# Two graph layers on one core: the adjacency transposed by DMA, an earlier load, and a new timetable

## The chip, the core and the metric

The kernel runs on one NeuronCore of a Trainium2 chip. Five engines with a queue each take part: TensorE (PE in the profile, its weight loads PEld) for matmuls and transposes, VectorE (DVE), ScalarE (ACT), GpSimd (POOL), and SyncE (SP), which here only issues DMAs. Each engine runs its own queue in order; an instruction that waits holds up everything behind it on that engine. The metric is the device time of one execution in microseconds, as a median of several runs. The profile is one execution of its own.

## What is computed

64 independent graphs, each with 256 nodes of 256 features and an integer adjacency matrix, go through two layers. The first is attention with relations: the softmax of q k is masked by each of four values of the adjacency, and each mask has its own values v. The second is a graph attention network with two attention steps that share the mask adjacency > 0. Both layers end in a feed-forward block. Cut to what matters here:

```python
# layer 0
scores = q @ k.T / sqrt(dh)                       # 8 heads of 32
attn = softmax(scores, axis=-1)
for r in range(4):
    out += (attn * (adj == r)) @ (src @ Wv[r])
x = ln(src + out @ Wo)
x = ln(x + gelu(x @ W1) @ W2)
# layer 1, the attention step twice
e = leaky_relu(Wh1 + Wh2.T)
h = softmax(where(adj > 0, e, -9e15), axis=1) @ Wh
x = ln(x + h);  x = ln(x + relu(x @ w_ff1) @ w_ff2)
```

## The kernel before

One graph is the unit of work: its 256 rows are two blocks of 128 partitions, and all its steps are methods of the class Graph, gathered by name in `operations`. All weights stay in SBUF. The matmuls are float32; the attention weights are used with the key nodes on the partitions, so the adjacency is needed transposed, too.

What sets the order is a timetable written out by hand. The dictionary PLACES gives each step a place; graph g has its steps at `g * PERIOD + place`, and the last lines of the kernel sort the steps of all 64 graphs by place and run them in that order, which is then each engine's queue order. A place is no time: it only ranks steps. With a period of 60 and places from about -14 to 270, steps of five graphs stand between each other. What is called place 33.7 below is a place taken modulo the period. A tile framework adds the semaphore waits and hands out the buffers: two of each front tile (`fp`), three PSUM tiles of the tag "mm", one PSUM bank for each of four heads' scores (`ps_s`).

The steps that the change and the prediction speak of:

- `load` (L134 to L139): the DMAs of x (xin) and of the adjacency (adi) of a graph, on SP. Graph 0's are issued first of all (L141), then come 34 DMAs of weights and vectors on the same queue (L142 to L177); all other loads come from the timetable. `y` (L433 to L435) loads x again for the residual, `store` (L524) writes the result; both are on SP as well.
- `cast` (L304, POOL) turns the integer adjacency into bfloat16 (adb). `jT` (L306 to L311) transposes it with four 128x128 transposes on TensorE into a PSUM tile, and `jTc` (L315, ACT) copies that to adT in SBUF. `mask0` to `mask4` (L326 to L331, POOL) compare adT with the relations; mask4 is the mask of the second layer.
- `xT` and `xTc` (L217, L221) transpose x; `qk0`, `qk1` (L337), `v00` to `v11` (L353) are the projections, in two halves m of four heads each.
- `s0`, `s1` (L370): scores of four heads as matmuls of 32 rows each[...]. Then for each head `max` (L375, DVE), `exp` (L383, ACT), `rec` (L388, DVE), `nrm` (L393, POOL), `eT` (L399, TensorE, back into the scores' PSUM bank), `es` (L404, ACT), `pm` (L408, DVE, the product with three masks), `pl` (L413, POOL, that with the last mask). `po0`, `po1` (L424) are the products with v, in matmuls of 32 columns.
- `wo` (L444), `ya`, then a layer norm of `st1` (DVE), `rt1` (L242, POOL) and `ln1` (L247, L251, DVE). The feed-forward block of the first layer: `aT`, `au0` to `au3` (L270), `ax0` to `ax3` (L277, ACT), `ad0` to `ad7` (L284), `ae` (L288, DVE), and its norm `st2`, `rt2`, `ln2`.
- `hT` (L217) transposes the result of ln2 for the second layer: `ga0`, `ga1` (L454), two attention steps (names in h and z), and a second feed-forward block with names in b, ended by `ln4` and `store`.

[...]

Of the kernel before, what the change touches and what calls it, by code (L numbers as in the profile page):

```python
# [12 lines left out]
BF16 = mybir.dt.bfloat16  # L13
# [4 lines left out]
P = 128  # L18
# [4 lines left out]

PERIOD = 60.0
PLACES = {
    "load": -13.81, "cast": -13.72, "xT": -4.66, "xTc": -4.31, "jT": -2.14, "jTc": 3.89, "qk0": 10.32,
    "qkc0": 15.38, "mask3": 18.4, "qk1": 19.52, "qkc1": 33.51, "mask0": 40.4, "v00": 41.99, "s0": 44.39,
    "max01": 45.28, "exp01": 46.53, "max00": 48.41, "exp00": 48.86, "vc00": 49.3, "max02": 50.12,
    "y": 51.75, "v10": 52.12, "max03": 52.91, "vc10": 53.45, "exp03": 53.62, "exp02": 54.7, "rec00": 55.23,
    "rec02": 56.39, "v11": 56.45, "rec03": 56.54, "mask1": 56.72, "mask2": 56.92, "nrm00": 57.02,  # L30
    "eT00": 57.47, "nrm03": 58.18, "vc11": 58.18, "es00": 58.93, "rec01": 61.34, "v01": 61.37,
    "nrm02": 62.41, "eT03": 62.5, "nrm01": 62.52, "pl00": 62.83, "eT02": 63.75, "pm00": 63.87, "eT01": 65,
    "es03": 65.49, "pl03": 66.47, "es02": 67.28, "vc01": 68.87, "es01": 69.64, "pl02": 70.44, "pm03": 70.48,
    "pm02": 71.62, "pm01": 72.69, "s1": 73.61, "pl01": 74.01, "max11": 74.9, "exp11": 76.55, "max10": 77.17,
    "exp10": 78.46, "max12": 78.53, "max13": 79.42, "rec11": 80.21, "po0": 80.41, "exp12": 82.35,
    "exp13": 82.95, "mask4": 83.04, "rec10": 83.25, "nrm10": 83.92, "rec12": 84.3, "rec13": 84.35,
    "nrm11": 86.8, "nrm13": 87.83, "nrm12": 88.42, "eT13": 89.04, "es13": 90.24, "eT11": 91.08,
    "eT10": 92.68, "oT0": 93.27, "es10": 95.39, "pm13": 95.55, "yb": 97.25, "eT12": 98.12, "pl13": 98.77,
    "es11": 99.15, "pl11": 99.64, "pm10": 101.39, "es12": 101.49, "pm11": 102.06, "pm12": 102.56,
    "pl10": 103.39, "pl12": 105.68, "po1": 105.84, "oT1": 109.02, "wo": 112.3, "ya": 114.97, "st1": 116.77,  # L40
    "rt1": 117.4, "ln1": 121.15, "aT": 123.26, "aTc": 126.48, "au0": 127.81, "au1": 127.98, "ax0": 130.26,
    "ax1": 130.8, "ad0": 134.18, "au2": 137.15, "ax2": 138.43, "au3": 139.03, "ax3": 139.66, "ad1": 140.92,
    "ad2": 141.77, "ad3": 145.91, "ad4": 145.97, "ar": 146.32, "ad5": 146.89, "ad6": 148.4, "ad7": 148.7,
    "ae": 150.15, "st2": 150.31, "rt2": 153.25, "ln2": 156.6, "hT": 159.27, "hTc": 159.41, "ga0": 159.97,
    "gac0": 160.28, "ga1": 161.37, "gac1": 161.98, "ipA": 162.06, "zA": 162.47, "zlA": 163.61,
    "zmA": 164.43, "zxA": 165.33, "zeA": 171.75, "zdA": 173.45, "h10": 176.82, "h1c0": 177.52,
    "h11": 177.66, "h1c1": 181.08, "ipB": 181.31, "zB": 181.33, "zlB": 185.72, "zmB": 187.61, "zxB": 187.79,
    "zeB": 189.32, "zdB": 191.16, "h2": 192.43, "h2a": 194.37, "st3": 195.73, "rt3": 199.46, "ln3": 203.48,
    "bT": 207.02, "bTc": 208.89, "bu0": 213.43, "bx0": 215.34, "bu1": 217.76, "bd0": 217.96, "bx1": 218.81,
    "bu2": 219.87, "bd1": 220, "bx2": 222.24, "br": 222.74, "bu3": 222.91, "bd2": 223.5, "bx3": 227.29,  # L50
    "bd3": 231.33, "bd4": 236.75, "bd5": 238.2, "bd6": 243.84, "bd7": 244.4, "be": 252.56, "st4": 253.99,
    "rt4": 257.67, "ln4": 265.08, "store": 269.91,
}


def _row(ap, n):

    return bass.AP(tensor=ap.tensor, offset=ap.offset, ap=[[0, P], [1, n]])
# [8 lines left out]
def kernel(  # L67
# [12 lines left out]
    nc = tc.nc  # L80
    B, N, D = x.shape
# [6 lines left out]
    C = N // P  # L88
# [4 lines left out]
    const = ctx.enter_context(tc.tile_pool(name="const", bufs=1))  # L93
# [8 lines left out]
    def mm_tile(shape, name, dt=F32):  # L102
        return ps_mm.tile(shape, dt, tag="mm", name=name)
# [4 lines left out]

    ident = const.tile([P, P], F32, name="ident")
    make_identity(nc, ident)  # L110
    ident_h = const.tile([P, P], BF16, name="ident_h")
    nc.vector.tensor_copy(ident_h, ident)
    nhalf = const.tile([P, 2], F32, name="nhalf")
    nc.vector.memset(nhalf, -0.5)
    negc = const.tile([P, 1], F32, name="negc")
# [2 lines left out]
    def weight(w, name):  # L118
        k, n = w.shape[0] // P, w.shape[1]
        t = const.tile([P, k, n], F32, name=name)  # L120
        nc.sync.dma_start(t, w.rearrange("(k p) n -> p k n", p=P))
        return t

    def rowvec(v, n, name):
        t = const.tile([P, n], F32, name=name)
        nc.sync.dma_start(t, _row(v, n))
        return t
# [6 lines left out]
    def load_front(g):  # L134
        xin = fp.tile([P, C, D], F32, tag="xin", name=f"xin{g}")
        nc.sync.dma_start(xin, x[g].rearrange("(c p) d -> p c d", p=P))
        adi = fp.tile([P, C, N], I32, tag="adi", name=f"adi{g}")
        nc.sync.dma_start(adi, adj[g].rearrange("(c p) d -> p c d", p=P))
        return xin, adi  # L139

    loaded = {0: load_front(0)}  # L141
# [8 lines left out]
    for m in range(KD):  # L150
        for k in range(KD):
            nc.sync.dma_start(
                wv[:, k, m], Wv[:, k * P:(k + 1) * P, m * P:(m + 1) * P].rearrange("r p n -> p r n"))
        nc.sync.dma_start(
            bv_r[:, m], bass.AP(tensor=bv.tensor, offset=bv.offset + m * P, ap=[[0, P], [D, R], [1, P]]))
    wo, bo_r = weight(Wo, "wo"), rowvec(bo, D, "bo_r")
    g1_r, be1_r = rowvec(g1, D, "g1_r"), rowvec(beta1, D, "be1_r")
    w1, b1_c = weight(W1, "w1"), colvec(b1, FF, "b1_c")
# [131 lines left out]
    class Graph:  # L290
# [12 lines left out]
            self.adb = fp.tile([P, C, N], BF16, tag="adb", name=f"adb{self.g}")  # L303
            nc.gpsimd.tensor_copy(self.adb, self.adi)  # L304

        def adj_product(self):  # L306
            self.ap = mm_tile([P, C, N], f"aT_ps{self.g}", BF16)
            for jc in range(C):
                for ic in range(C):
                    nc.tensor.transpose(self.ap[:, jc, ic * P:(ic + 1) * P],  # L310
                                        self.adb[:, ic, jc * P:(jc + 1) * P], ident_h)  # L311

        def adj_copy(self):
            self.adT = fp.tile([P, C, N], BF16, tag="adT", name=f"adT{self.g}")
            nc.scalar.copy(self.adT, self.ap)  # L315

        def mask(self, r):

# [207 lines left out]
        def operations(self):  # L526

            g, ops = self.g, {}
# [5 lines left out]
            ops["cast"] = self.cast  # L534
            ops["xT"] = lambda: self.xt.product(self.xin)
            ops["xTc"] = self.xt.copy
            ops["jT"] = self.adj_product
            ops["jTc"] = self.adj_copy
            for r in range(R + 1):
                ops[f"mask{r}"] = lambda r=r: self.mask(r)  # L540
            for m in range(KD):
# [56 lines left out]
    for g in range(B):  # L598
        ops = Graph(g).operations()
# [34 lines left out]
```

## Time and profile before

| | |
|---|---|
| timed runs, us | 4013.57, 4013.96, 4015.55; median 4013.96 |
| profiled execution: span, us | 4008.9 |
| granted TensorE clock | 0.994 of full speed |
| distance between the jT steps of two graphs in the middle, us | 61.31 |
| DMA | 80.00 MB, 20 GB/s over the span |
| load of xin or adi, median us to landing | 2.9 and 3.2 |
| four bfloat16 transposes of L310, per record | 219 ns, 256 records |
| copy of L315 on ACT | 586 ns, 64 of them |
| loads of a function table on ACT | 381, 1283 ns each |

A line of the profile names the engine, the source line, the operation, what it writes and reads, the shape, and how many there are, then the busy time and the mean of one; behind the bar stands the idle time of the engine just before, and what ended it. In a timeline, the first column is the start and the second the duration in microseconds, and equal instructions that follow each other are merged into one line with their number; a bracket gives the idle time before it and its cause. A float32 matmul appears as two MATMUL records, a transpose as one. Matmuls are pipelined, so the duration of one record (some 380 ns for 256 columns) is longer than the distance to the next (216 ns); the distance between starts is what counts. The busy slices cut the span into 40 equal parts of about 100 us, each with a digit in tenths.

### The profile page before, as it was taken

To read this page: it belongs to the slowest core of one execution; us is meant where nothing else is said; L and a number is where in the kernel's file an instruction comes from. 1 tells how busy PE (TensorE), PEld (TensorE's weight loads), DVE (VectorE), ACT (ScalarE), POOL (GpSimd) and SP (SyncE) were. 2 spreads that over 40 slices of the span, in tenths; PEclk is the share of its full clock that TensorE was granted. 3 is DMA by queue.
4 is the path that set the end of the run, shared out by engine and by line. 5 is a ranking of instruction groups with operands and counts; after the bars stand their busy time and mean duration, and the time that the engine had idled before them with its cause. 6 is when DMAs were issued, how large, how long until landed. Compare 5 with 4: busy or idle time off the path is not lost.

```text
span 4008.9 us, 67819 instructions
## 1 busy us (share of the span) xinstructions
PE 3945.9 (98%) x26136; PEld 3026.2 (75%) x26136; DVE 2788.9 (70%) x5129; ACT 2321.4 (58%) x5693; POOL 2154.9 (54%) x2374
## 2 busy tenths in 40 slices
PE   6999999999999999999999999999999999999998
PEld 4677777777777777777777777777777777777776
DVE  4677667676776776777767767767777677677675
ACT  3565565565655655656656556556566565565563
POOL 4555555555555555555555555555555555555551
PEclk8999999999999999999999999999999999999999
DMA  4000000000000000000000000000000000000000
GB/s 112 11 22 12 22 16 18 22 12 22 22 12 22 22 12 22 13 21 22 12 22 22 11 22 22 12 22 12 22 22 12 22 22 12 22 22 12 22 6 11
DMA packets 82404, 80.00 MB, mean 20 GB/s; under 512 B 8224, under 2 KB 81568, under 8 KB 82080
## 3 DMA queue, kind: packets, MB, share of 16 engines
q1 hardware_dynamic: 82080, 75.66, 6.2%
q8 instruction: 206, 3.38, 0.4%
q14 instruction: 118, 0.97, 0.1%
HBM read 58.87 MB, written 16.78 MB: 19 GB/s over the span
## 4 chain that ended last, share of the span: by engine, by line
PE 60%; ACT 16%; DVE 10%; issue 6%; POOL 4%; POOLq 0%; DVEq 0%; ACTq 0%
PE v_ps L353 11%; PE ffb_po L284 10%; ACT e L383 6%; PE po L424 6%; PE ffa_ps L270 6%; PE ffb_ps L270 5%; ACT L383 4%; ACT L277 4%; POOL e L393 4%; PE s L370 3%; PE ga_wps L454 3%; DVE pm L408 3%; PE wo_ps L444 3%; PE h_ps L503 3%; PE qk_ps L337 3%
## 5 line engine op out<-in xcount | busy, mean ns | idle before, releaser
L393 POOL TENSOR_SCALAR e<-e,rden 128x256 f32<-128x256 f32 x1024 | 588.4, 589 | 896.6 <-ACT xT L221 597.9
L408 DVE TENSOR_TENSOR pm<-rel,s 128x1536 f32<-128x1536 uint8 x512 | 887.0, 1743 | 55.9 <-ACT es L404 55.8
L413 POOL TENSOR_TENSOR pm<-rell,es 128x512 f32<-128x512 bf16 x512 | 609.4, 1201 | 225.2 <-ACT es L404 225.2
L383 ACT ACTIVATE e<-s,nmax 128x256 f32<-128x256 f32 x1024 | 474.0, 473 | 318.2 <-DVE nmax L375 316.7
L242 POOL TENSOR_TENSOR rs_x<-ve_x,nhalf 128x2 f32<-128x2 f32 x256 | 183.7, 718 | 691.4 <-DVE ve_x L238 673.7
L284 PE MATMUL ffb_po<-f,ffb_h 128*128 128x256 f32 x2048 | 524.1, 384 | 0.0
L284 PE MATMUL ffa_po<-w,ffa_h 128*128 128x256 f32 x2048 | 486.5, 385 | 0.0
L353 PE MATMUL v_ps<-wv,xT 128*128 128x512 f32 x1024 | 484.6, 596 | 0.0
L270 PE MATMUL ffb_ps<-ffb_T,f 128*128 128x256 f32 x2048 | 475.4, 380 | 0.7 <-ACT ffb_T L221 0.7
L424 PE MATMUL po<-pm,v 128*32 128x256 f32 x8192 | 469.8, 381 | 0.0
L270 PE MATMUL ffa_ps<-ffa_T,w 128*128 128x256 f32 x2048 | 463.2, 379 | 0.0
L284 PEld LDWEIGHTS ffb_po<-f,ffb_h 128*128 128x128 f32 x2048 | 374.3, 190 | 95.4 <-issue 29.6
L284 PEld LDWEIGHTS ffa_po<-w,ffa_h 128*128 128x128 f32 x2048 | 373.8, 190 | 90.0 <-issue 46.8
L404 ACT COPY es<-s 128x512 f32<-128x512 f32 x512 | 301.8, 590 | 222.5 <-PE s L399 181.4
L270 PEld LDWEIGHTS ffa_ps<-ffa_T,w 128*128 128x128 f32 x2048 | 384.2, 190 | 49.8
L375 DVE TENSOR_REDUCE nmax<-s 128x2 f32<-128x512 f32 x512 | 333.5, 683 | 111.5 <-PE s L370 111.5
L270 PEld LDWEIGHTS ffb_ps<-ffb_T,f 128*128 128x128 f32 x2048 | 375.5, 191 | 44.6 <-ACT ffb_T L221 1.1
L424 PEld LDWEIGHTS po<-pm,v 128*32 128x32 f32 x8192 | 253.4, 110 | 197.6 <-issue 44.1
L388 DVE RECIPROCAL rden<-den 128x2 f32<-128x2 f32 x512 | 69.3, 156 | 353.4 <-ACT e L383 353.3
L360 DVE TENSOR_TENSOR v<-v_ps,bv_r 128x512 f32<-128x512 f32 x256 | 175.6, 686 | 199.4 <-PE v_ps L353 191.2
L331 POOL TENSOR_SCALAR rel<-adT 128x512 uint8<-128x512 bf16 x192 | 310.1, 1625 | 0.0
L399 PEld LDWEIGHTS s<-ident,e 128*128 128x128 f32 x2048 | 245.4, 141 | 62.3 <-issue 18.7
(108 smaller groups left out, 6362.9 us busy)
## 6 DMA issues: line engine op xcount, KB each, us to landing
xin<-in_x_dram SPq DMA_DIRECT2D x64, 256.0 KB, 2.9
adi<-in_adj_dram SPq DMA_DIRECT2D x64, 256.0 KB, 3.2
y<-in_x_dram SPq DMA_DIRECT2D x64, 256.0 KB, 3.7
out_dram<-ffb_res SPq DMA_DIRECT2D x64, 256.0 KB, 2.2
w<-in_L_gnn_W_dram SPq DMA_DIRECT2D x2, 1024.0 KB, 8.6
f<-in_L_gnn_w_ff_dram SPq DMA_DIRECT2D x2, 1024.0 KB, 9.3
wv<-in_L_gnn_Wv_dram SPq DMA_DIRECT2D x4, 256.0 KB, 5.1
bv_r<-in_L_gnn_bv_dram SPq DMA_DIRECT2D x2, 256.0 KB, 5.5
```

Source lines behind the costliest of these rows:

```text
L270: nc.tensor.matmul(p[:, f - f0, :], self.wa[:, k, f * P:(f + 1) * P], self.x.t[:, k, :], start=(k == 0), stop=(k == KD - 1))
L284: nc.tensor.matmul(self.p[:, c, :], self.h[:, f, c * P:(c + 1) * P], self.wb[:, f, :], start=(f == 0), stop=(f == KF - 1))
L331: nc.gpsimd.tensor_scalar(self.rel[:, r], self.adT, float(r), None, op0=ALU.is_equal)
L353: nc.tensor.matmul(p, self.xt.t[:, k, jc * P:(jc + 1) * P], wv[:, k, m].rearrange("p r n -> p (r n)"), start=(k == 0), stop=(k == KD - 1))
L375: nc.vector.tensor_reduce(self.nmax[m, h], self.s4[m][h].rearrange("p (c n) -> p c n", c=C), AX.X, ALU.max, negate=True)
L383: nc.scalar.activation(e[:, ic, :], self.s4[m][h][:, ic * N:(ic + 1) * N], AF.Exp, bias=self.nmax[m, h][:, ic:ic + 1], accum_out=self.den[ ...
L393: nc.gpsimd.tensor_scalar(e[:, ic, :], e[:, ic, :], self.rden[m, h][:, ic:ic + 1], 1.0, op0=ALU.mult, op1=ALU.mult)
L399: nc.tensor.transpose(self.s4[m][h][:, jc * N + ic * P:jc * N + (ic + 1) * P], self.e[m, h][:, ic, jc * P:(jc + 1) * P], ident)
L404: nc.scalar.copy(self.es[m, h], self.s4[m][h])
L408: nc.vector.tensor_tensor(self.pm[m, h], self.rel.rearrange("p r c n -> p r (c n)"), bc(self.s4[m][h], [P, R - 1, C * N]), ALU.mult)
L413: nc.gpsimd.tensor_tensor(self.pm_l[m, h], self.rel_l.rearrange("p c n -> p (c n)"), self.es[m, h], ALU.mult)
L424: nc.tensor.matmul(po[hp, :], self.v[m][:, jc, r, hp], w, start=(r == 0 and jc == 0), stop=(r == R - 1 and jc == C - 1))
```

## The change

Three things change at once.

1. The four transposes on TensorE and the copy on ACT become two DMA transposes on SP, each from one block of 128 rows of adb straight to its columns of adT. The step jTc no longer exists, nor does the bfloat16 identity matrix.
2. x and the adjacency of graph 1 are loaded ahead of wo, that is, after the weights of the projections and before all later ones.
3. All 175 places of the timetable are new. No step but jT and jTc changes what it does.

```diff
-    ident_h = const.tile([P, P], BF16, name="ident_h")
-    nc.vector.tensor_copy(ident_h, ident)
...
+    loaded[1] = load_front(1)
     wo, bo_r = weight(Wo, "wo"), rowvec(bo, D, "bo_r")
...
-        def adj_product(self):
-            self.ap = mm_tile([P, C, N], f"aT_ps{self.g}", BF16)
-            for jc in range(C):
-                for ic in range(C):
-                    nc.tensor.transpose(self.ap[:, jc, ic * P:(ic + 1) * P],
-                                        self.adb[:, ic, jc * P:(jc + 1) * P], ident_h)
-
-        def adj_copy(self):
+        def adj_transposed(self):
             self.adT = fp.tile([P, C, N], BF16, tag="adT", name=f"adT{self.g}")
-            nc.scalar.copy(self.adT, self.ap)
+            for ic in range(C):
+                nc.sync.dma_start_transpose(out=self.adT[:, :, ic * P:(ic + 1) * P], in_=self.adb[:, ic, :])
...
-            ops["jT"] = self.adj_product
-            ops["jTc"] = self.adj_copy
+            ops["jT"] = self.adj_transposed
```

Of the timetable, the places that the prediction speaks of, before and after, modulo the period of 60 where they stand in it:

| step | before | after | | step | before | after |
|---|---|---|---|---|---|---|
| load | 46.2 | 40.9 | | s1 | 13.6 | 13.6 |
| store | 29.9 | 52.9 | | po0 | 20.4 | 14.9 |
| cast | 46.3 | 49.3 | | ad7 | 28.7 | 29.9 |
| jT | 57.9 | 55.3 | | ae | 30.2 | 31.2 |
| y | 51.8 | 58.2 | | pm13 | 35.5 | 36.5 |
| mask3 | 18.4 | 10.6 | | ln2 | 36.6 | 33.7 |
| s0 | 44.4 | 46.8 | | hT | 39.3 | 35.5 |
| po1 | 45.8 | 48.3 | | ln4 | 25.1 | 29.4 |

Between s1 and po0 stood ad0, au2, au3 and qk1 before; now nothing does. In the order before, pm13 stood on DVE between st2 and ln2; now ln2 follows st2 directly.

## The prediction

> **What bounds the kernel now.** I read the busy table first, then the busy slices, then TensorE's timeline of one graph in the middle, then the start, then the Vector engine (DVE) beside a place where TensorE waits.
>
> ```profile
> PE 3945.9 (98%) x26136; PEld 3026.2 (75%) x26136; DVE 2788.9 (70%) x5129; ACT 2321.4 (58%) x5693; POOL 2154.9 (54%) x2374
> ...
> PE   6999999999999999999999999999999999999998
> ```
>
> TensorE is busy in every slice but the first and the last; no other engine is over 70%. A busy TensorE need not be at its peak, so the next view is the timeline of TensorE around one graph, with start, duration, and how many records were merged:
>
> ```profile
> 2009.27 0.60 PE L217 MATMUL ffb_T_ps<-ident,ffa_res 128*128 128x128 f32 x4
> 2009.70 1.89 PE L284 MATMUL ffa_po<-w,ffa_h 128*128 128x256 f32 x8
> 2011.43 1.47 PE L399 MATMUL s<-ident,e 128*128 128x128 f32 x12
> ...
> 2017.06 0.60 PE L399 MATMUL s<-ident,e 128*128 128x128 f32 x4
> 2017.67 0.94 PE L217 MATMUL hT_ps<-ident,ffa_res 128*128 128x128 f32 x4
> 2018.45 1.89 PE L270 MATMUL ffb_ps<-ffb_T,f 128*128 128x256 f32 x8
> ...
> 2041.69 0.39 PE L310 MATMUL aT_ps<-ident_h,adb 128*128 128x128 bf16 x4
> 2041.92 1.08 PE L284 MATMUL ffb_po<-f,ffb_h 128*128 128x256 f32 x4
> 2042.84 0.38 PE L466 MATMUL gb_ips<-ident,gb_wh 128*128 128x128 f32 x2
> ...
> 2055.25 1.15 PE L370 MATMUL s<-kT,qT 32*128 32x256 f32 x16
> 2056.33 1.13 PE L284 MATMUL ffa_po<-w,ffa_h 128*128 128x256 f32 x4
> 2057.30 3.62 PE L270 MATMUL ffa_ps<-ffa_T,w 128*128 128x256 f32 x16
> ```
>
> The distance from start to start is what a group costs. Every group follows on the last with no hole, so in the middle a microsecond taken off TensorE is a microsecond of time. But three costs stand inside the groups. Eight plain records take 1.73 us (2009.70 to 2011.43), so four take 0.86. The four of 2041.92, after the bfloat16 transposes, take 0.92; the four of 2056.33, after the tiled scores, 0.97. And hT's four transposes take 0.78 where ffb_T's four take 0.43, with 0.61 for the four before them: hT waits 0.35 + 0.17 = about 0.52 us per graph. The start has one long hole:
>
> ```profile
> 16.85 1.98 PE L353 MATMUL v_ps<-wv,xT 128*128 128x512 f32 x4
> 39.33 1.09 PE L217 MATMUL xT_ps<-ident,xin 128*128 128x128 f32 x4 [20.49 <-DMA xin<-in_x_dram]
> ```
>
> The second graph's x is issued behind all weights, at 32.64 in SP's timeline. GpSimd (POOL) has the same hole, for the second adjacency, and then two masks before the first normalisation (L393) at 43.50:
>
> ```profile
> 40.01 0.61 POOL L304 CAST adb<-adi 128x512 bf16<-128x512 int32 x1 [27.94 <-DMA adi<-in_adj_dram]
> 40.58 2.94 POOL L331 TENSOR_SCALAR rel<-adT 128x512 uint8<-128x512 bf16 x2
> 43.50 3.67 POOL L393 TENSOR_SCALAR e<-e,rden 128x256 f32<-128x256 f32 x8
> ```
>
> What hT waits for is in DVE's timeline ahead of it: the mask product (L408) stands between the statistics and ln2 (L247, L251), whose last instruction ends at 2018.01.
>
> ```profile
> 2013.49 1.75 DVE L408 TENSOR_TENSOR pm<-rel,s 128x1536 f32<-128x1536 uint8 x1
> 2015.16 2.06 DVE L247 SCALAR_TENSOR_TENSOR ffa_res<-ffa_res,mv_x,g_r 128x256 f32<-128x256 f32 x2
> 2017.14 0.87 DVE L251 SCALAR_TENSOR_TENSOR ffa_res<-ffa_res,rs_x,be_r 128x256 f32<-128x256 f32 x2
> ```
>
> [...] The trace has 219 ns per TensorE record, and 56 ns from start to start; it has no DMA transpose. [...] SP stood 3711.6 us in front of the stores of L524. [...] the last full record before the scores or L424 takes 309 ns in place of 216, and the first after them 320. [...] L247 on ffa_res takes from 476 to 1391 ns.
>
> **The change, part by part.**
>
> (1) Four bfloat16 transposes per graph leave TensorE. They cost 2041.92 - 2041.69 = 0.223 us, and the record after them loses 0.056 (272 ns in place of 216). 64 x 0.279 = 17.9 us, all on the path.
>
> (2) The copy of aT_ps on ACT goes: 64 x 0.586 = 37.5 us. ACT's new order also needs 255 loads of a function table where it had 381: 126 x 1.283 = 162 us. ACT is at 58%, behind TensorE's work: nothing. The bfloat16 identity goes as well; it kept L310 until 7.78, but the long hole of the start absorbs that: nothing.
>
> (3) 128 DMA transposes of 64 KB are added on SP. Each issue costs SP about 0.47 us, as its plain ones do, or a few times that; SP idles through most of each period. [...] Who waits: cast is at place 49.3 of the period and mask3 at 70.6; the TensorE groups between these places (v10 to qk0) sum to about 19 us by their starts. So in the middle it is hidden, by TensorE's own work: nothing. SP's order in a period is now load, store, the two transposes, y; it was store, load, y. The transposes wait for cast; behind them stand y (read by yb 40 places later) and the load of the next graph but one (read by its cast some 50 places later). Ahead of them stands the store, whose ln4 (29.4) is long done when cast (49.3) is. Nothing waits for any of these: nothing.
>
> (4) New places. On TensorE, s1 and po0 now stand side by side, as s0 and po1 did before, so there are two tiled blocks per graph and not three. One entry (309 - 216 = 93 ns) and one exit from scores (320 - 216 = 104) go: 0.197 x 62 graphs = 12.2 us. The ends are 0 and this.
>
> (5) On DVE, ln2 (33.7) now stands ahead of the mask product pm13 (36.5), so its chain from ae is 1.67 us shorter (2013.49 to 2015.16), and TensorE still has as much between ad7 and hT (bu0, eT13, qk1, eT11, bu1: 6.05 us, before 6.06). The wait is 0.52, so it should go: 0.51 x 61 = 31.1 us. Ends: 0, if ln2 starts later for another reason, and 31.
>
> (6) The start. The load of x and adj for graph 1 moves ahead of wo, so the hole before xT goes. But graph 0's transposes are issued by SP after all weights, at what was the place of y, about 33.6 and 34.2 us, and POOL has mask3 of graph 0 at its head: nothing behind it can run. x, issued at 32.64, was there at 39.33, 6.7 us later; the same gives 40.8 for the second transpose (ends 36.5 at a quiet 2.9 us[...]). Then POOL runs mask3, mask0, mask1, cast and mask2 = 1.5 + 1.5 + 1.5 + 0.6 + 1.5 = 6.6 us, and the first normalisation starts at 47.4, before at 43.50. The hole moves from xT to eT00 and grows by 3.9 us; a microsecond comes back since v11 is now done before it. I take +3 us (ends -1[...]). The drain at the end I take as unchanged (within 2).
>
> The sum is -17.9 - 12.2 - 31.1 + 3 = -58.2 us. In the profile's own span that is 4008.9 to 3950.7; the median of the timed runs is 5.1 above that span, so 4013.96 becomes **3956 us**.
>
> **Rivals.** A, the wait of hT stays or another takes its place: for it speaks that every place of the timetable is new and L247 varies threefold[...]; against it, 1.1 us of room. It gives 4014 - 17.9 - 12.2 + 3 = 3987. B, transposes crawl behind the weights, and the start loses some 15 us more: for it speaks that bf_r (26.18 in SP's timeline) kept SP for 5.47 us there; against it, that little is queued after it. It gives 3971. C, slower: the pair of transposes is late for mask3 in every graph. The place is POOL's queue, where the normalisations and products that TensorE needs stand behind mask3; the point is about 19 us from cast to landing plus the few that POOL can catch up, say 25. From there each microsecond costs up to one per graph: at 27 us, 2 x 62 = 124, so 3956 + 124 = 4080. Nothing in the trace shows a DMA transpose, so this can't be excluded[...]. D, another order brings new waits of 0.95 us per graph that just cancel it.
>
> **Chances.** The forecast 0.70, A 0.12, B 0.08, C 0.07, D 0.03. Faster and slower mean by over 0.2%, 8 us, about what a measurement of this kernel can tell. So faster is 0.70 + 0.12 + 0.08 = 0.90, same 0.03, slower 0.07. The range: low from the best ends (-17.9 - 12.2 - 31.1 - 1 - 2 = -64, with something for waits that I don't see in the drain) 3944; high 3986, which holds B and leaves out C, D and half of A.
>
> **What would show it.** No aT_ps on TensorE; hT's four at 0.44 us; two groups of scores and po side by side, with two entries of 309 ns per graph; periods of 61.31 (from one graph's aT_ps to the next) - 0.99 = 60.3 us; the long hole before eT00, ended by POOL's L393, POOL's own by the DMA of adT[...]. I am wrong if POOL's mask3 waits for a DMA in the middle, or if TensorE gets a new wait there.

## The result and the profile after

| | before | after |
|---|---|---|
| median of 6 timed runs, us | 4014.11 (4013.18 to 4015.55) | 3950.06 (3949.34 to 3951.59) |
| ratio | 1 | 0.9841, 95% interval 0.9828 to 0.9853 |
| profiled execution: span, us | 4008.9 | 3949.8 |
| period: xT of one graph to xT of the next, mean over graphs 5 to 60, us | 61.307 | 60.326 |
| rest: span less 63 periods, us | 146.6 | 149.3 |

The forecast was 3956 us. The profiled spans differ by 59.1 us, the sum of the prediction by 58.2. The medians differ by 64.05, 5 us more, since single runs of one kernel lie a few microseconds apart and the profile is one of them: the profiled run of the kernel before took 4010.73, 3.4 below its median, that of the changed kernel 3951.59, 1.5 above. The last two rows split the 59.1: 63 x 0.981 = 61.8 us come from the period, and 2.7 us are lost in what is left, the filling of the pipeline and its drain. All experiments below are read by these two numbers, because they separate what happens in each graph from what happens once. The rest of a single profile is good to some 3 us, as the last part shows.

In the page of the changed kernel, the busy table, the busy slices, the shares of the chain and the DMA issue answer to the lines of before:

```profile
PE 3887.5 (98%) x25880; PEld 3012.9 (76%) x25880; DVE 2810.7 (71%) x5128; ACT 2097.2 (53%) x5503; POOL 2169.1 (55%) x2374
...
PE   6999999999999999999999999999999999999998
...
PE 96%; DVE 2%; issue 1%; SPq 1%; POOL 0%; ACT 0%; DMA 0%; POOLq 0%; DVEq 0%; ACTq 0%
...
adT<-adb SPq DMA_TRANSPOSE x128, 2.3
```

TensorE has 256 records less (the transposes), is still busy in every slice but the ends, and now holds 96% of the chain of waits, where it held 60% before. ACT fell by 224 us and the time did not follow it: ACT was hidden. The last line says how long a DMA transpose takes from issue to landing, 2.3 us in the median. The timeline of TensorE around one graph (start, duration, records merged):

```profile
2023.76 1.15 PE L363 MATMUL s<-kT,qT 32*128 32x256 f32 x16
2024.84 3.66 PE L417 MATMUL po<-pm,v 128*32 128x256 f32 x64
2028.43 1.13 PE L283 MATMUL ffa_po<-w,ffa_h 128*128 128x256 f32 x4
2029.39 3.62 PE L269 MATMUL ffa_ps<-ffa_T,w 128*128 128x256 f32 x16
...
2045.83 0.60 PE L216 MATMUL hT_ps<-ident,ffa_res 128*128 128x128 f32 x4
2046.27 1.89 PE L269 MATMUL ffb_ps<-ffb_T,f 128*128 128x256 f32 x8
...
2056.53 1.15 PE L363 MATMUL s<-kT,qT 32*128 32x256 f32 x16
2057.61 3.66 PE L417 MATMUL po<-pm,v 128*32 128x256 f32 x64
```

hT's four transposes take 2046.27 - 2045.83 = 0.44 us where they took 0.78. Scores and po stand next to each other in both places. The reason for hT is in DVE's timeline, where ln2 (L246, L250) now ends at 2044.66, 1.2 us before hT starts, and the mask product (L401) comes after it:

```profile
2040.70 0.75 DVE L233 BATCH_NORM_STATS2 st_x<-ffa_res 128x6 f32<-128x256 f32 x2
...
2041.78 0.88 DVE L246 SCALAR_TENSOR_TENSOR ffa_res<-ffa_res,mv_x,g_r 128x256 f32<-128x256 f32 x2
2042.87 1.79 DVE L250 SCALAR_TENSOR_TENSOR ffa_res<-ffa_res,rs_x,be_r 128x256 f32<-128x256 f32 x2 [0.22 <-POOL rs_x L241]
2044.58 6.74 DVE L401 TENSOR_TENSOR pm<-rel,s 128x1536 f32<-128x1536 uint8 x4
```

The view of the tile hT_ps counts the idle times ahead of hT that DVE's ffa_res ended, over the whole run (sum in us, times), first for the kernel before and then for the changed one:

```profile
  DVE ffa_res L251: 41.9, 130
...
  DVE ffa_res L250: 6.9, 8
```

This view adds the idle times of the weight loads to those of the matmuls, so its sum only says whether hT waits; what a wait costs is read from the period.

The start still has its long hole, in another place. First TensorE, then POOL:

```profile
15.40 3.70 PE L346 MATMUL v_ps<-wv,xT 128*128 128x512 f32 x8
46.35 1.36 PE L392 MATMUL s<-ident,e 128*128 128x128 f32 x4 [27.24 <-POOL e L386]
```

```profile
4.39 0.61 POOL L303 CAST adb<-adi 128x512 bf16<-128x512 int32 x1 [3.10 <-DMA adi<-in_adj_dram]
39.38 1.52 POOL L322 TENSOR_SCALAR rell<-adT 128x512 bf16<-128x512 bf16 x1 [34.38 <-DMA adT<-adb]
...
45.81 3.68 POOL L386 TENSOR_SCALAR e<-e,rden 128x256 f32<-128x256 f32 x8
```

The adjacency of graph 0 is in bfloat16 at 5.0 us. In SP's timeline its transposes are issued at 34.51, behind the last weight vector, and POOL, with mask3 at the head of its queue, is idle for 34.38 us until they land. In the middle nothing of this is left. These are SP and then POOL around one graph there:

```profile
1753.30 2.46 SPq L308 DMA_TRANSPOSE adT<-adb  x2
```

```profile
1752.67 0.60 POOL L303 CAST adb<-adi 128x512 bf16<-128x512 int32 x1
...
1771.69 2.29 POOL L406 TENSOR_TENSOR pm<-rell,es 128x512 f32<-128x512 bf16 x2
1773.95 1.50 POOL L322 TENSOR_SCALAR rell<-adT 128x512 bf16<-128x512 bf16 x1
```

The second transpose is issued by 1754.5 and takes 2.3 us more, so it has landed near 1757. mask3 follows its neighbour on POOL at 1773.95 with no idle time in front of it: 20.7 us after the cast has ended.

### The profile page after: what moved, and what is told of

Read it like the earlier page. It is cut to its first block, busy times and chain, and to the rows that moved or that the text cites. A ratio compares the mean times of both kernels' runs of the same rounds, so it can differ in the third digit from the quotient of the medians.

```text
span 3949.8 us, 67437 instructions
## 1 busy us (share of the span) xinstructions
PE 3887.5 (98%) x25880; PEld 3012.9 (76%) x25880; DVE 2810.7 (71%) x5128; ACT 2097.2 (53%) x5503; POOL 2169.1 (55%) x2374
## 4 chain that ended last, share of the span: by engine, by line
PE 96%; DVE 2%; issue 1%; SPq 1%; POOL 0%; ACT 0%; DMA 0%; POOLq 0%; DVEq 0%; ACTq 0%
PE po L417 12%; PE ffa_po L283 11%; PE v_ps L346 11%; PE ffa_ps L269 11%; PE ffb_ps L269 11%; PE ffb_po L283 11%; PE s L392 6%; PE qk_ps L330 5%; PE s L363 3%; PE ga_wps L447 3%; PE h_ps L496 3%; PE wo_ps L437 3%; PE h_ps L510 3%; PE hT_ps L216 1%; PE ffb_T_ps L216 1%; PE ffa_T_ps L216 1%
## 5 line engine op out<-in xcount | busy, mean ns | idle before, releaser
L386 POOL TENSOR_SCALAR e<-e,rden 128x256 f32<-128x256 f32 x1024 | 628.6, 626 | 851.0 <-DVE rden L381 847.1
L401 DVE TENSOR_TENSOR pm<-rel,s 128x1536 f32<-128x1536 uint8 x512 | 867.3, 1742 | 30.3 <-ACT es L397 30.3
L368 DVE TENSOR_REDUCE nmax<-s 128x2 f32<-128x512 f32 x512 | 347.3, 680 | 482.3 <-PE s L363 482.3
L241 POOL TENSOR_TENSOR rs_x<-ve_x,nhalf 128x2 f32<-128x2 f32 x256 | 194.8, 761 | 774.0 <-DVE ve_x L237 667.4
L283 PE MATMUL ffb_po<-f,ffb_h 128*128 128x256 f32 x2048 | 503.9, 379 | 0.0
L269 PE MATMUL ffb_ps<-ffb_T,f 128*128 128x256 f32 x2048 | 485.8, 380 | 0.7 <-ACT ffb_T L220 0.7
L392 PEld LDWEIGHTS s<-ident,e 128*128 128x128 f32 x2048 | 254.7, 142 | 130.8 <-POOL e L386 51.6
L276 ACT ACTIVATE ffa_h<-ffa_ps,b_c 128x256 f32<-128x256 f32 x512 | 214.8, 471 | 249.2 <-PE ffa_ps L269 248.4
L276 ACT ACTIVATE ffb_h<-ffb_ps,bf_c 128x256 f32<-128x256 f32 x512 | 215.3, 474 | 243.2 <-PE ffb_ps L269 243.2
L392 PE MATMUL s<-ident,e 128*128 128x128 f32 x2048 | 309.4, 274 | 28.7 <-POOL e L386 28.3
```

The costliest lines, as they stand in the source:

```text
L269: nc.tensor.matmul(p[:, f - f0, :], self.wa[:, k, f * P:(f + 1) * P], self.x.t[:, k, :], start=(k == 0), stop=(k == KD - 1))
L276: nc.scalar.activation(self.h[:, f, :], self.ps[f0][:, f - f0, :], self.func, bias=self.ba[:, f:f + 1])
L283: nc.tensor.matmul(self.p[:, c, :], self.h[:, f, c * P:(c + 1) * P], self.wb[:, f, :], start=(f == 0), stop=(f == KF - 1))
L368: nc.vector.tensor_reduce(self.nmax[m, h], self.s4[m][h].rearrange("p (c n) -> p c n", c=C), AX.X, ALU.max, negate=True)
L386: nc.gpsimd.tensor_scalar(e[:, ic, :], e[:, ic, :], self.rden[m, h][:, ic:ic + 1], 1.0, op0=ALU.mult, op1=ALU.mult)
L392: nc.tensor.transpose(self.s4[m][h][:, jc * N + ic * P:jc * N + (ic + 1) * P], self.e[m, h][:, ic, jc * P:(jc + 1) * P], ident)
```

## The experiments

The first theory: the period is shorter by three terms that add up (transposes off TensorE, s1 next to po0, ln2 ahead of pm13), the DMA transposes are hidden in the middle with much room, and at the start they pay back what the early load gains. The rivals: one of the terms does not carry, the DMA transposes cost something in the middle, or the start is bound by the weights anyway.

### DMA transposes alone

The kernel before, with its places and its late load, and jT as in the changed kernel:

```diff
...
-            ops["jT"] = self.adj_product
-            ops["jTc"] = self.adj_copy
+            ops["jT"] = self.adj_transposed
```

> The kernel before with the DMA transposes alone: no transposes on TensorE, old places otherwise, late load. Theory: 0.279 us less per graph (period 61.31 - 0.28 = 61.03, 17.9 us in all), the wait of hT stays at about 0.5 us and there are still three tiled blocks; at the start the first normalisation moves from 43.5 to about 45 us, +2: 4013 - 18 + 2 = 3997 (3993 to 4001). Rival (the transposes themselves bring most of the 64 us, by a lighter ACT, TensorE and PSUM): 3975 or less.

Measured: 3998.08 us (3996.17 to 3999.54), ratio 0.9965 (0.9952 to 0.9978). The period is 61.033, or 0.274 less, where the working said 0.279. The rest is 152.7, 6 more, where about 2 were expected; single profiles scatter by some 3, and the difference is not explained. hT waits as before, which its tile's view shows (records, then the sum and number of idle times ahead of them):

```profile
L215 PE MATMUL hT_ps<-ident,ffa_res x256: 272/328/473, 124.7 to 3943.4; 128*128 128x128 f32 x128
...
  DVE ffa_res L249: 41.3, 130
```

So the first term stands, and taking ACT's copy away does nothing to DVE's chain.

### The mask product back ahead of ln2

The changed kernel with one place undone:

```diff
-"pm13": 96.51,
+"pm13": 93.3,
```

> The changed kernel with pm13 at place 93.3 in place of 96.5, so that it stands on DVE between st2 and ln2 again. Theory (ln2's place ahead of pm13 is what closed the wait of hT): hT waits again, 0.3 to 0.8 us per graph, so 19 to 50 us: 3969 to 4000, with hT the only new wait on TensorE. Rival (ACT's lighter load or the lack of a PSUM tile closed it): within 6 us of 3949.

Measured: 3987.05 us (3986.06 to 3987.84), 37.0 more than the changed kernel; period 60.878, 0.552 more. The same view:

```profile
  DVE ffa_res L250: 72.6, 131
```

The waits are back. By this view they are longer than before (72.6 against 41.9), by the distances of TensorE's starts only a little: around hT 0.55 us are lost per graph, where the kernel before loses 0.51 and the changed one nothing. Nothing else in the order moved, so this one place carries over half of what the period gained.

### po0 away from s1

The changed kernel with po0 at 77.5, so that ad0 stands between s1 and po0:

```diff
-"po0": 74.9,
+"po0": 77.5,
```

> The changed kernel with po0 behind ad0 (place 77.5 in place of 74.9), so that ad0 stands between s1 and po0 and there are three tiled blocks per graph. Theory: one entry of 93 ns and one exit of 104 ns more, period 60.33 + 0.20 = 60.52, 12 us in all: 3949 + 12 = 3961 (3957 to 3965). Rival (switches are hidden in the durations, or moving po0 opens a wait): under 3953 or over 3968.

Measured: 3961.86 us (3958.53 to 3964.04), 11.8 more than the changed kernel; period 60.523, 0.197 more, which is what was worked out. TensorE's timeline of this kernel:

```profile
2028.90 1.03 PE L330 MATMUL qk_ps<-xT,wk 128*128 128x256 f32 x4
2029.86 1.15 PE L363 MATMUL s<-kT,qT 32*128 32x256 f32 x16
2030.94 1.13 PE L283 MATMUL ffa_po<-w,ffa_h 128*128 128x256 f32 x4
2032.00 3.66 PE L417 MATMUL po<-pm,v 128*32 128x256 f32 x64
```

The four records of qk_ps last 0.96 us to the next start and those of ffa_po 1.06; four plain ones take 0.86. The change from plain records to tiled ones (of 32 rows or 32 columns) and back is paid around each block of this trace: about 0.1 going in and 0.1 coming out. From s to po, both tiled, nothing is added that the period shows.

### The transposes back on TensorE, all else new

The changed kernel with its places and early load, but jT (place 0.5) and jTc (place 3.0) as before:

```diff
...
-            ops["jT"] = self.adj_transposed
+            ops["jT"] = self.adj_product
+            ops["jTc"] = self.adj_copy
```

> The changed kernel with the transposes back on TensorE (jT at place 0.5, the copy jTc on ACT at 3.0), new places and early load kept. Theory: each graph costs 0.279 us more in the middle (period 60.33 + 0.28 = 60.6; 17.9 us in all), but the start loses its hole, about -24 us: 3950 + 18 - 24 = 3944 (3938 to 3952). Rival (the lighter ACT and PSUM are what closed the wait before hT): the wait of hT is back, period about 61.1, time 3970 or more.

Measured: 3947.7 us (3944.72 to 3949.13), ratio 0.9836 (0.9819 to 0.9852). That cannot be told from the changed kernel, yet both halves differ: the period is 60.720, 0.394 more, and the rest is 122.0, 27.3 less. hT waits no more than in the changed kernel (6.9 us in 8 times by its tile's view), so the rival that ACT's missing copy or the freed PSUM tile closed that wait falls. TensorE in the middle:

```profile
2056.22 0.39 PE L311 MATMUL aT_ps<-ident_h,adb 128*128 128x128 bf16 x4
2056.45 0.38 PE L467 MATMUL gb_ips<-ident,gb_wh 128*128 128x128 f32 x2
2056.74 1.98 PE L354 MATMUL v_ps<-wv,xT 128*128 128x512 f32 x4
2058.56 0.60 PE L400 MATMUL s<-ident,e 128*128 128x128 f32 x4
```

The period's 0.394 is the 0.23 of the four transposes, about 0.07 more for the two gb_ips (0.29 against 0.22 in the changed kernel), and 0.10 for v_ps (1.82 against 1.72). I had expected 0.28. The return from bfloat16 cost about 0.17 with gb_ips and v_ps behind the transposes, three times the 0.056 of the old place.

So, with the new places and the early load, DMA transposes bring 63 x 0.394 = 24.8 us in the periods and take 27.3 us at the start. Beside the other two parts of the change they brought nothing on balance.

### Only the early load, and only without it

The line `loaded[1] = load_front(1)` added to the kernel before, and then taken out of the changed kernel:

> The kernel before with one edit: graph 1's load ahead of wo; transposes on TensorE, old places. Theory (the old hole was that load alone, and with transposes on TensorE nothing takes its place): the hole of 20.5 us before xT shrinks to under 3, time 4014 - 20 = 3994 (3990 to 3998). Rival (weights' traffic): 4010 or more.

> The changed kernel with graph 1's load back at its place in the timetable, behind the weights. Theory (in the changed kernel the early load gains nothing, since the first transposes are later anyway): the transposes of graph 0 come about 1 us earlier, the time stays within 4 us of 3950. Rival (the early load is worth the 20 us of the old hole): about 3970.

Measured: 3988.2 us (3987.81 to 3990.27), 25 less than the kernel before beside it (4013.2), for the first; period 61.313, rest 125.8, that is 20.8 less. The profile has the 20 that were expected, the median 5 more, just beyond the expected range. For the second, 3948.94 us (3946.86 to 3951.88), ratio 0.9842 (0.9827 to 0.9857), no difference from the changed kernel: period 60.326, rest 144.5. With TensorE's transposes the early load closes the hole. With DMA transposes behind the weights it does not matter, since the hole before eT00 is there either way. So the changed kernel takes the same time without its early load as it takes without its DMA transposes (3948.94 and 3947.7). From the early load alone (3988.2) to the early load with the new places (3947.7) it is 40.5 us: on this path the 64 us are 25 from the load and some 40 from the places. In the first, the first transpose of e comes at 21.19:

```profile
18.51 0.60 PE L218 MATMUL xT_ps<-ident,xin 128*128 128x128 f32 x4
...
21.19 1.01 PE L400 MATMUL s<-ident,e 128*128 128x128 f32 x4 [0.36 <-POOL e L394]
```

### The start: transposes among the weights

The changed kernel with graph 0's cast and two transposes issued right behind the early load, ahead of wo; then also graph 1's, ahead of gw1. The timetable's own cast and jT of these graphs then do nothing:

```diff
     loaded[1] = load_front(1)
+    transpose_early(0)        # cast on POOL, two dma_start_transpose on SP
...
     wo, bo_r = weight(Wo, "wo"), rowvec(bo, D, "bo_r")
...
+    transpose_early(1)        # in the second kernel alone
```

> The changed kernel with one edit: the cast and the two DMA transposes of graph 0 stand right behind the early load of graph 1, ahead of wo and all later weights. Theory (the hole of the start has only moved: graph 0's transposes wait behind 34 loads on SP, and POOL's mask3 waits for them): adT of graph 0 lands at about 15 us in place of 39.4, the first normalisation comes at about 22 us in place of 45.8, and the time falls by 12 to 24 us, to 3926 to 3938, the rest being taken by graph 1's transposes, which still wait behind the weights. Rival (the weights' own traffic sets the start, whatever the order): within 4 us of 3950.

> The changed kernel, but graph 0's cast and transposes are issued right behind the early loads and ahead of wo, and graph 1's right behind that part of the weights and ahead of gw1, not behind all weights. In the run with graph 0's alone, mask3 of graph 1 then waited 12.2 us for its transposes (issued at 36.7) and TensorE's po lost 7.5 us to it. Theory: that wait goes, the first transposes of hT come 7 to 12 us earlier than with graph 0's alone (there at 103.3), and the time is 3920 to 3930. Rival: TensorE was held by the arrival of the weights or by DVE in that stretch anyway, or SP's wait for the cast delays the weights behind it; then 3932 to 3940, no better than graph 0's alone.

Measured: 3934.44 us (3933.17 to 3936.19), ratio 0.9806 (0.9791 to 0.982), for graph 0's alone. The period is unchanged at 60.326, the rest 132.4, 16.9 less. mask3 of graph 0 starts at 14.92 in place of 39.38. But mask3 of graph 1 now waits, and TensorE's po with it (POOL, then TensorE):

```profile
41.87 1.50 POOL L332 TENSOR_SCALAR rell<-adT 128x512 bf16<-128x512 bf16 x1 [12.23 <-DMA adT<-adb]
```

```profile
44.54 3.04 PE L427 MATMUL po<-pm,v 128*32 128x256 f32 x14 [7.53 <-POOL pm L416]
```

With graph 1's as well: 3925.05 us (3923.24 to 3926.53), ratio to the kernel before 0.9782 (0.9766 to 0.9798), and 25 us below the changed kernel, whose own runs stood beside a kernel before of the same time (4013.82 and 4014.11). Period 60.326, rest 120.9. POOL, then TensorE, of this kernel:

```profile
14.71 1.52 POOL L338 TENSOR_SCALAR rell<-adT 128x512 bf16<-128x512 bf16 x1
...
28.80 1.50 POOL L338 TENSOR_SCALAR rell<-adT 128x512 bf16<-128x512 bf16 x1
```

```profile
21.11 1.36 PE L408 MATMUL s<-ident,e 128*128 128x128 f32 x4 [2.43 <-POOL e L402]
...
33.00 3.66 PE L433 MATMUL po<-pm,v 128*32 128x256 f32 x64
```

No mask waits for a transpose any more, and po runs without a hole. The rest is what it is with TensorE's transposes (122.0), so the whole price of the DMA transposes at the start came from their place on SP's queue. The rival, that the weights bound this stretch anyway, falls.

### How late may the transposes be?

To see the rival that would have been slower, the changed kernel issues each pair of transposes 4, 8, 10 and 12 times from the third graph on, the same data again:

```diff
-            for ic in range(C):
+            for ic in (range(C) if self.g < 2 else 4 * list(range(C))):   # then 8, 10, 12
```

> The changed kernel with each pair of transposes issued four times over, one after the other, for all graphs but the first two: the same data is written to the same place, so the output is unchanged. From the end of cast to the start of mask3 the changed kernel's trace has 20.7 us, and a pair lands about 4.8 us after the cast. Theory (hidden by this window): the eight take about 12 to 16 us, mask3 waits for none, time within 4 us of 3949. Rival (transposes disturb the other engines or queues as they run): at least +0.1 us per graph, 3956 or more.

> From the third graph on, each pair of transposes is issued eight times over (the same data again), so SP is at it for 16 x 1.45 = 23 us per graph (1.45 us each, as the run with four repeats showed), and the last lands some 2.3 us later: 25.5 us after cast, where the time from cast to mask3 is 20.7 us in the median. So mask3 must wait about 5 us in every graph. My theory (slack behind the wait): POOL is at 55% and catches up, so the period stays within 60.33 to 60.6 us and the time within 3950 to 3968. Rival C of the prediction at its full price (TensorE pays each microsecond of the wait from some point on): up to 4 us per graph, period above 62, time above 4050. If mask3 does not wait at all, the repeats overlap better than those of four did, and the run says nothing on the point.

> As the run with eight repeats, but ten (20 transposes per graph, the same data again, from the third graph on). There SP took 21.63 us for 16, the last landed so that mask3 started 22.9 us after cast's end, waiting 2 to 3 us in each graph, at no cost. Twenty take 27 us, so mask3 starts 28.3 us after cast's end. In the trace of the changed kernel the two products behind mask3 on POOL end 5.7 us before the po that reads them starts (1777.8 to 1783.5), and mask3 starts 20.7 us after cast, so TensorE should begin to pay at 26.4 us. Theory: each microsecond beyond that point costs TensorE one per graph: 1.9 x 62 = 118 us, a period of 62.2, a time of 4065 (4010 to 4090), and the wait is seen at po. Rival (the queues catch up, other work of TensorE fills in): period below 60.6, time below 3965.

> As before, with twelve repeats (24 transposes, 32.5 us on SP): mask3 starts 33.7 us after cast's end, 7.3 us beyond the point of 26.4. Theory: 7.3 x 62 = 450 us, a period of 67.6, a time of 4400 (4250 to 4450); if the longer period itself also delays the next cast against mask3, the cost per microsecond is one and not more. Rival (partly caught up): the period grows by under half of that, time below 4170.

| times issued | SP in one graph, us | end of cast to mask3, median us | time, us | period, us |
|---|---|---|---|---|
| 1 | 2.46 | 20.7 | 3950.06 | 60.326 |
| 4 | 11.60 | 20.7, no wait | 3951.78 (3947.38 to 3953.8) | 60.326 |
| 8 | 21.63 | 23.4 | 3948.33 (3947.65 to 3949.11) | 60.326 |
| 10 | 26.91 | 29.0 | 3977.23 (3974.84 to 3981.13) | 60.608 |
| 12 | 33.23 | 34.6 | 4433.52 (4427.2 to 4435.59) | 68.016 |

With four and eight the mean DMA traffic rises from 22 GB/s to 29 and 37, and TensorE's period does not change by a nanosecond: the transposes as such cost TensorE nothing here. With eight, mask3 waits in every graph, 212.0 us in all by the view of adT, at no cost either. With ten I expected 4065 and got 3977; with twelve I expected 4400 and got 4434. Why the ten missed can be read off TensorE with twelve, in one graph:

```profile
1798.67 1.15 PE L363 MATMUL s<-kT,qT 32*128 32x256 f32 x16
1799.75 3.21 PE L417 MATMUL po<-pm,v 128*32 128x256 f32 x50
1807.48 0.62 PE L417 MATMUL po<-pm,v 128*32 128x256 f32 x2 [4.52 <-POOL pm L406]
1808.60 1.92 PE L417 MATMUL po<-pm,v 128*32 128x256 f32 x12 [0.50 <-POOL pm L406]
1810.45 2.08 PE L283 MATMUL ffa_po<-w,ffa_h 128*128 128x256 f32 x4
```

po starts without the late products and runs 50 of its 64 records, some 2.8 us, before it needs the first of them. I had counted the room to po's start, so the point is not at 26.4 us but near 29.2. The twelve agree: the two starts around their hole at record 50 lie 4.25 us apart in the mean over 50 graphs, which with mask3 at 34.6 puts the point at 30.3 for the first product; the second comes 1.1 us later and is wanted 0.1 later (two records), which makes it 29.3. With ten, at 29.0 in the median, only some graphs are beyond it (the longest has 30.9); in their trace po shows no delay in any graph up to 29.0, and from 29.1 on the delay grows. That the twelve came within their range is luck: the point was taken nearly 3 us too early and the price of a microsecond too low, and the two nearly cancel.

From 29.3 to 34.6 there are 5.3 us to wait, but the period grew by 7.7. The table of windows of the same kernel shows where the rest of it went (the stretch, its length, TensorE's busy time and records, its granted clock, the DMA share, GB/s); the first five lines are the graph just shown, the last three another one with a hole of 3.8 us:

```profile
1799.00:1807.00 8.00, 3.96 (x66) 1.00 0.48 130
1807.00:1810.00 3.00, 2.02 (x14) 0.67 0.03 8
1810.00:1813.00 3.00, 3.00 (x10) 0.50 0.00 0
1813.00:1817.00 4.00, 4.00 (x15) 0.77 0.00 0
1817.00:1821.00 4.00, 4.00 (x22) 1.00 0.00 0
...
1873.00:1876.30 3.30, 0.00 (x0) 1.00 0.64 196
1876.30:1879.30 3.00, 2.91 (x15) 0.50 0.00 0
1879.30:1881.00 1.70, 1.70 (x9) 0.88 0.00 0
```

Behind these holes of 4.5 and 3.8 us TensorE has half its clock. The figures between 0.50 and 1.00 are means of windows that hold some of each, so the second graph's lines make 3.4 us at half clock, which lose 1.7 us, and the first's 6.8 us, which lose 3.4. In the trace's clock record from 300 to 3700 us, 50 graphs, there are 50 such stretches, 40 of 6.83 us and ten of 3.41. So per graph TensorE is idle for 4.0 us and loses 3.1 to the clock, which accounts for 7.1 of the 7.7. A wait that reaches TensorE costs more than itself here, and my "one and not more" fell as well. With ten it holds: from 300 to 3700 us no hole is longer than 0.5 us, the clock stays at 1.00, and a period longer by 0.28 us stands against a mean of 0.26 us beyond 29.1.

The hole of 3.8 us was followed by 3.41 us at half clock, that of 4.5 us by twice as much. The shortest of these 50 holes is 2.6 us, and the clock was halved behind it, too. Over the whole run the mean granted clock is 0.95, where the changed kernel has 0.994. My expectation had not counted the clock.

## Why the prediction was right

The sum came out at -58.2 against -59.1 in the profile, and its parts hold one by one. Between the medians it is -64.05, and the forecast was 6 us too high: it added 5.1 us to the profiled span, the distance that one profile of the kernel before had from the median, while the changed kernel's median lies 0.3 above its span. That last step was no reading of the kernel but of one run.

**(1) Transposes off TensorE, 0.279 per graph.** Right: 0.274 when done alone. It is no constant of the operation: put elsewhere, the same four cost 0.394.

**(2) ACT's copy and table loads, nothing.** Right as far as the runs reach: ACT lost 224 us. Its loads of a function table, 1283 ns each, fell from 381 to 255; in the kernel before, 190 of them stand at the line with the gelu (L277) and 189 at that with the exp (L383), in the changed one 127 and 126. And the three terms of TensorE as measured by themselves (0.274 + 0.197 + 0.552 = 1.02) leave nothing of the period's 0.981 for ACT. They are 0.04 above it; what takes that back is open. The table loads were not tried by themselves.

**(3) DMA transposes hidden in the middle.** Right. SP pays 1.17 to 1.27 us per issue, which is the "few times" 0.47 that was allowed for. A DMA with two 128x128 blocks lands in 2.3 us in the median, where a plain load of xin takes 3.2, so the pair is there 3.6 us after cast. How soon the pair lands was not shown by the trace of the kernel before, which has no DMA transpose; the argument needs only that it lands inside the window, which was put at 19 us and is 20.7.

**(4) s1 beside po0, 0.197.** Right: 0.197 when undone. The entry and the exit were priced from the trace, at 93 and 104 ns, and undoing the place gave them back.

**(5) ln2 ahead of pm13, 0.51.** Right: around hT the starts of the kernel before lose 0.51 us per graph and those of the changed kernel nothing, and putting pm13 back cost 0.552. Rival A, that another wait would take its place, fell: 1.2 us of room where 1.1 had been read. D, new waits of 0.95 us per graph, is excluded by the period.

**(6) The start, +3 us.** The hole moved to eT00 as said. mask3 started on the landed transposes at 39.38 (40.8 predicted), the first normalisation came at 45.81 (47.4). The rest grew by 2.7, but the rests of the kernels with this same start lie between 146.8 and 151.5 (but for 160.7 of the ten repeats, whose period varies from graph to graph), so a step of 3 us is within what single profiles scatter: the sign is not shown by this pair alone. Rival B, 15 us more, is excluded. What the prediction did not see is how much was there to be had: it took the early load as given and counted the difference, 3 us, where the load was worth 21 to 25 us and the place of the transposes cost 27. The trace before showed the first as the hole of 20.49 us, and it showed that the transposes would have only SP's queue ahead of them: POOL's cast of graph 0 ended there at 4.9 us.

**Rival C**, the late mask, had the right place. Its point is at 29.3 us and not at 25, and beyond it a microsecond costs about one while the holes are short, as with ten, and about 1.5 with twelve (7.7 for 5.3). But the real pair lands 3.6 us after cast, in a window of 20.7, far from the point. The chance of 0.07 was the author's estimate; the trace of the kernel before could not support one, since it has no DMA transpose.

## What to carry to other kernels

Split a time into periods and a rest, and price each edit in both: here the early load and the transposes by DMA each gain alone (25 and 14 us), yet taking either one out of the changed kernel costs nothing, because the transposes open again at the start the hole that the load closes. A DMA that takes work over from an engine comes in the order of the queue that issues it: behind the weights, POOL waited 34.38 us for it at the start, and the kernel with both graphs' transposes among the weights took 25 us less. So put it where its input is ready, not where its timetable step happens to fall behind the weights. With eight repeats, POOL, busy for 55% of the changed kernel, waited 212.0 us for the transposes at no cost; with ten and twelve repeats it cost time beyond 29.1 and 29.3 us after cast, where the reader of its result ran dry. Count such a point to the record that reads the result, not to the start of its group.

## What was not expected of the hardware

- Four bfloat16 transposes between float32 work cost more than themselves: 0.056 us for the four records behind them in the old place, about 0.17 in another.
- A DMA transpose of 64 KB from SBUF to SBUF holds SP's queue for 1.2 us, 2.6 times a plain DMA of this kernel (0.47); issued one after another, 16 of them took 21.63 us in one graph, 1.35 each.
- How much the clock adds to a hole that recurs: 5.3 us of waiting cost 7.7 in each graph, since behind the holes, 2.6 us and longer, the clock was at half for 3.41 or 6.83 us in every one of 50 graphs. The ten's holes of up to 0.5 us left it at full.
